# Two-level Strassen GEMMs on one core: accumulators c and d in one double bank, a new slot order and a lag of two ticks

## Chip, cores and metric

The kernel runs on one core of one Trainium2 chip. The metric is the device time of one execution in microseconds (us); the time of a kernel is the median of several runs.

## What is computed

One transformer layer over x of 8 batches x 512 tokens x 1024 features, all in float32. It has causal attention with 16 heads and rotary embedding, and a feed-forward GEMM with a LoRA term; each is wrapped in a LayerNorm before and a LayerNorm behind, and added to its input:

```python
x = x + ln(attention(ln(x)))        # q,k,v = h@Wq, h@Wk, h@Wv; rotary; causal softmax; out @ Wo
y = einsum('bsd,od->bso', ln(x), weight) + bias
lo = einsum('bsr,bor->bso', einsum('bsd,brd->bsr', ln(x), A), Bw)   # adapter by batch
x = x + ln(y + where(use_lora, lo, 0))
```

## The kernel before

The work goes through four stages. **V** (0 to about 430 us) normalizes x and multiplies it by Wv, batch by batch. The **attention** stage (about 431 to 1676 us) makes q and k, the scores, the softmax and its product with v; it has its own class `Product` (L93) and its own order PRODUCTS. **O** (about 1676 to 2020 us) multiplies by Wo, and **F** (about 2020 to 2471 us) is the feed-forward GEMM. In the program V's batches are numbered q = -8 to -1, O's 0 to 7 and F's 8 to 15.

*A batch as 49 products.* V, O and F use one scheme. The 512x1024 by 1024x1024 GEMM of a batch is computed by a two-level Strassen method: seven GROUPS (L51) at the outer level, named P1 to P7 after Strassen's products, and in each group seven sub-products SUBS, named P1 to P7 again. So a batch has N2 = 49 products. ORDER (L61) is the order of the groups in a batch, P1, P2, P4, P5, P7, P6, P3; LAST (L62) is that of the very last batch. SLOTS is the order of the seven sub-products in a group.

*Operands.* The left factors L11 to S4 are weight tiles and their sums; in V they are made on chip, for O and F they are loaded (`load_sums`, from sums made on GpSimd at L567). The right factors R11 to R22 and T1 to T4 come from the data: in V by LayerNorm (`stats_x`, `norm_x`), a transpose on TensorE (`transpose_x`, tile `ptx`, L454) and a copy on ScalarE (`keep_x`); in O and F by DMA (`load_right`). T1, T2, T4 and T3 are differences of R's, made by `sum_right` (L275) in three pieces each, on GpSimd mostly. They are written over older R's whose readers are done (`next_roles`): a batch's last group, P3, reads the last of them.

*Accumulators.* Within a group P1 and P2 accumulate into a PSUM tile a, P6 and P7 into b, P5 and P3 into c, P4 into d (SUBS). A tile is 128x256 float32. ACCS gives the buffers: a 1 (2 in O and F), b 2, c 2, d 1. `Group.product` (L302ff) opens a tile at its first product and issues two matmuls (L320, four records in the profile); in F some groups add a LoRA matmul (L327). `Group.drain` (L339ff) takes the results out: after P1 ScalarE copies a to p1 and VectorE makes u2 = b + p1; after P7 VectorE makes p1 += b, then the output quarters c + p1 and d + p1; after P2 ScalarE copies a; after P3 VectorE makes c + u2 (L342 are VectorE's adds, L347 and L354 ScalarE's copies). So TensorE's P3 adds to a c that VectorE has read in P7's drain just before. The products of slots run P6, P1, P3 of the group before, P5, P4, P7, P2: P3 of a group comes in the third slot of the next one.

*The order by hand.* `products` (L370) goes through ticks; one tick is one product. At each tick `run` (L176) issues first the events of kind "pe", then the product, then the drain of the tick before, then the other events of the tick in the order in which they were planned. Each engine takes its instructions in this order. The events are planned at fixed ticks relative to a batch's first tick, `base`: `plan_x` (V: load, statistics, norm and transposes of the next batch), COMBINE and the list in the loop over q (sums of whole groups on VectorE and GpSimd, L360), `store_v`, `plan_right` (loads and sums of the next batch's right factors), `plan_left` (F's weights, during O's last batch), `plan_rows` (O and F: row loads, the LayerNorm of the output rows, the add to the residual on GpSimd at L1109, stores, and in O a second LayerNorm with transposes on VectorE at L1118) and `plan_last` (the last batch). Loads and stores are issued on SyncE's queue (SP). O's first three groups (AHEAD) are computed in the attention stage.

*PSUM.* V uses six banks for the accumulators and two for transposes, O and F seven and one.

Of the kernel before, what the change touches and what calls it, by code (L numbers as in the profile page):

```python
# [10 lines left out]
F32 = mybir.dt.float32  # L11
# [6 lines left out]
P = 128  # L18
B, S, E = 8, 512, 1024
# [43 lines left out]
SUB = 256  # L63
# [8 lines left out]
    "P6": ("S2", "T2", "b"),  # L72
    "P7": ("S3", "T3", "b"),
}
SLOTS = ["P6", "P1", "P3", "P5", "P4", "P7", "P2"]

QK = {"P1": "A", "P2": "B", "P6": "D", "P7": "E", "P4": "F", "P5": "D", "P3": "E"}
ACCS = {"a": 1, "b": 2, "c": 2, "d": 1}
SLOT_L = {"L11": 0, "L12": 1, "S3": 2, "L22": 3, "S1": 4, "S2": 5, "S4": 6}
SLOT_R = {"R11": 0, "R21": 1, "T3": 2, "R22": 3, "T1": 4, "T2": 5, "T4": 6}  # L80

# [51 lines left out]
def sandwich_kernel(  # L133
# [161 lines left out]
    class Group:  # L295
# [9 lines left out]
        def product(self, p):  # L305
            l, r, a = SUBS[p]
            first = a not in self.acc
            if first:
                self.acc[a] = env["acc"].tile(
                    [P, SUB], F32, tag=a, bufs=2 if a == "a" and self.q >= 0 else ACCS[a], name=f"acc{a}_{self.name}"  # L310
                )
            acc = self.acc[a]
            left, right = self.W[self.L], RX[self.q, self.R][:, SLOT_R[r]]
            for k in range(2):
                stays = right[:, k, :] if self.q < B else by_blocks(right, k)
                if self.q < 0:
                    moving = left[:, SLOT_L[l], k, :]
                else:
                    moving = left[:, 4 * k : 4 * k + 4, SLOT_L[l], :]
                nc.tensor.matmul(  # L320
                    acc, lhsT=stays, rhs=moving,
                    start=(first and k == 0), stop=True, skip_group_check=True,
                )
            if self.lora and p in LORA_SUB:
                half, cols = self.lora
                i, c = LORA_SUB[p]
                nc.tensor.matmul(  # L327
                    acc, lhsT=hts[self.q - B][:, cols[c], :],
                    rhs=env["lb"][:, half * HALF + i * SUB : half * HALF + (i + 1) * SUB],
                    start=False, stop=True, skip_group_check=True,  # L330
                )
# [7 lines left out]
        def drain(self, p):  # L339

            acc, t = self.acc, self.t
            add = lambda out, x, a: nc.vector.tensor_tensor(out, acc[a], x, op=ALU.add)  # L342
            if p == "P1":
                env["u2"].reverse()
                for n, pool in (("p1", env["p1"]), ("u2", env["u2"][0])):
                    t[n] = pool.tile([P, SUB], F32, tag=n, name=f"{n}_{self.name}")
                nc.scalar.copy(t["p1"], acc["a"])  # L347
                add(t["u2"], t["p1"], "b")
            elif p == "P7":
                add(t["p1"], t["p1"], "b")  # L350
                add(self.dest(1, 1), t["p1"], "c")
                add(self.dest(1, 0), t["p1"], "d")
            elif p == "P2":
                nc.scalar.copy(self.dest(0, 0), acc["a"])  # L354
            elif p == "P3":
                add(self.dest(0, 1), t["u2"], "c")
# [13 lines left out]
    def products(q0, count, order, first=0):  # L370


        cur, before, todo = None, None, None

        def fill(q, g, p):
            nonlocal cur, before, todo
            if p == 0:
                before = cur
                cur = Group(q, order(q)[g]) if q < q0 + count else None
            name = SLOTS[p]  # L380
            group = before if name == "P3" else cur
            if group:
                group.product(name)
            if todo:
                todo[0].drain(todo[1])
            todo = (group, name) if group else None

        for n in range(first, count * N2 + 4):
            q, m = divmod(n, N2)
            g, p = divmod(m, NP)  # L390
            run(n, lambda q=q, g=g, p=p: fill(q0 + q, g, p))
# [80 lines left out]

    def plan_x(b, base):

        at(base + 10, next_roles)
        for t in range(NT):
            at(max(0, base - 12) + t, lambda t=t: load_x(b, t))
            k = (4, 5, 17, 19)[t]
            for m in range(4):
                at(base + k + m, lambda t=t, m=m: stats_x(b, t, m))  # L480
            at(base + k + 4, lambda t=t: norm_x(b, t))
        for n, k in (("R11", 11), ("R21", 18), ("R12", 25), ("R22", 32)):
            g, h = int(n[1]) - 1, int(n[2]) - 1
            for c in range(2):
                t = 2 * h + c
                at(base + k + c, lambda t=t, g=g: transpose_x(b, t, g), "pe")
                at(base + k + c, lambda pt, t=t, g=g: keep_x(b, t, g, pt), "post")
            at(base + k + 3, lambda n=n: sub_right(b - B, n, pool))
        for n, k in (("T1", 38), ("T2", 45), ("T4", 52), ("T3", 63)):
            eng = dve if n in ("T1", "T3") else pool  # L490
            for m in range(3):
                at(
                    base + k + (m if eng is dve else 0),
                    lambda n=n, m=m, eng=eng: sum_right(gvp, b - B, n, eng, slice(m, m + 1)),
                )
        for n, k in (
            ("R11", 18), ("R21", 25), ("R22", 40), ("T1", 44), ("T2", 54), ("T4", 60), ("T3", 69)
        ):
            at(base + k, lambda n=n: store_operand(b, n))
# [42 lines left out]
    for b in range(B):  # L542
        base = b * N2
        if b + 1 < B:
            plan_x(b + 1, base)
        for k, *op in COMBINE:
            at(base + k, lambda b=b, op=op: combine(b - B, *op[1:], op[0]))
        for k, tag, half, h in ((22, "c11", 0, 0), (53, "c21", 1, 0), (54, "c12", 1, 1), (57, "c22", 0, 1)):
            at(base + k, lambda b=b, tag=tag, half=half, h=h: store_v(b, tag, half, h))


    def plan_sums(pool, name, src, dst, ticks, eng=nc.gpsimd):
# [508 lines left out]
    with ExitStack() as a:  # L1061
# [88 lines left out]
            )  # L1150

        def plan_right(q, base):

            if q > 1:
                at(base + 6, next_roles)
            for n, k in (("R11", 10), ("R21", 17), ("R12", 24), ("R22", 31)):
                if q == 1 and n != "R22":
                    continue
                at(base + k, lambda n=n: load_right(gp, q, n))
                if q >= B:  # L1160
                    at(base + k + 4, lambda n=n: sub_right(q, n, nc.gpsimd, slice(0, 3)))
            if q >= B:
                for h, k in ((0, 25), (1, 39)):
                    at(base + k, lambda h=h: lora_in(q - B, h), "pe")
                    at(base + k, lambda ph, h=h: lora_keep(q - B, h, ph), "post")
                    for g in range(2):
                        at(base + k, lambda n=f"R{g + 1}{h + 1}": sub_right(q, n, nc.vector if h else nc.gpsimd, slice(3, 4)))
                at(base + 42, lambda: sub_ht(q - B))
            for n, k in (("T1", 40 if q == 1 or q >= B else 38), ("T2", 46 if q >= B else 45), ("T4", 52), ("T3", 63)):
                eng = nc.vector if q >= B and n in ("T1", "T3") else nc.gpsimd  # L1170
                for m in range(3):
                    at(
                        base + k + (m if eng is nc.vector else 0),
                        lambda n=n, m=m, eng=eng: sum_right(gp, q, n, eng, slice(m, m + 1)),
                    )

        def plan_left(base):


            for n, k in zip(("L11", "L12", "L22", "S1", "S3", "S2", "S4"), (10, 22, 34, 46, 56, 64, 72)):  # L1180
                pool = wop2 if n in ("S3", "S2", "S4") else wop
                at(base + k, lambda n=n, pool=pool: load_sums(pool, "wf", n, n))

        def plan_rows(q, base):

            for t in range(NT):
                k = base + 55 + 7 * t
                key = f"{'o' if q < B else 'y'}{q}_{t}"
# [59 lines left out]
        for q in range(NQ):  # L1248
# [4 lines left out]
                plan_left(base)  # L1253
            dve, pool = nc.vector, nc.gpsimd
            for k, e, res, l, r in (
                (18, dve, "c11", "c11", "A"), (38, pool, "c21", "c21", "c12"), (45, dve, "U", "U", "A"),
                (46, dve, "c22", "c22", "U"), (47, pool, "c21", "c21", "U"),
                (48, dve, "c12", "c12", "c22"), (52, dve, "c22", "c22", "A"),
            ) if q + 1 < NQ else (
                (18, dve, "U", "U", "A"), (31, dve, "c12", "c12", "U"), (33, dve, "U", "U", "c22"),  # L1260
                (34, pool, "c22", "c22", "c12"), (39, pool, "c11", "c11", "A"),
                (45, dve, "c21", "c21", "c12"),
            ):
                if base + k >= AHEAD:
# [100 lines left out]
```

## Time and profile before

| | us |
|---|---|
| median of 3 runs | 2475.75 |
| lowest and highest | 2475.05 and 2478.72 |
| the profiled execution | 2473.42 |
| its span | 2471.3 |

The mean granted TensorE clock of the span is 0.992. Busy times (share of the span):

| TensorE matmul | VectorE | ScalarE | GpSimd |
|---|---|---|---|
| 2361.4 us (96%) | 1782.8 us (72%) | 1046.1 us (42%) | 1518.8 us (61%) |

PE is TensorE's matmuls, PEld its weight loads, DVE VectorE, ACT ScalarE, POOL GpSimd, SP SyncE. A line `PE ptx L454 <- ACT x L420` in a list of waits means that a TensorE instruction of line 454, writing tile ptx, waited for ScalarE's write of x in line 420. In a timeline a row gives start, duration, engine, line, operation, output, inputs and shapes; a matmul's duration is modelled and overlaps with the next, so the distance between starts is the better measure.

### The profile page before, as it was taken

Reading aid. Unit: us, or ns where it says so; the run is one execution under the profiler, and the core shown is the slowest. Engines: PE = TensorE matmul, PEld = TensorE weight load, DVE = VectorE, ACT = ScalarE, POOL = GpSimd, SP = SyncE. Lnnn points to the kernel's source line nnn. Section 1 sums busy time; section 2 is a strip of 40 time slices with the busy share of each in tenths; the row PEclk is TensorE's granted clock in tenths of the full one; section 3 lists DMA queues with packets and bytes.
Section 4 is the critical chain, followed back from the end, with each engine's and each line's share of the span. In section 5 each row is a group of like instructions: output and inputs, shape, how many; then the busy total and the mean of one; then the engine's idle time right before and its main releaser. Section 6 shows DMA issues by size and latency. Waiting matters only on the chain. (4 is left out here: it accounts for less than half of the span.)

```text
span 2471.3 us, 37151 instructions
## 1 busy us (share of the span) xinstructions
PE 2361.4 (96%) x11936; PEld 1860.6 (75%) x11936; DVE 1782.8 (72%) x3942; ACT 1046.1 (42%) x2650; POOL 1518.8 (61%) x1125
## 2 busy tenths in 40 slices
PE   6999999999999999999999999799999988999997
PEld 4787887886677777777777776458888877888886
DVE  8777767384857759576685866776989988766676
ACT  3323331125555555555565566652434333222223
POOL 3878875204364553735646364776887886777674
PEclk8999999999999999999999999999999999999999
DMA  7697787998999897988989897467777698444433
GB/s 263 196 302 247 245 268 231 349 298 260 272 297 289 247 338 246 313 299 279 324 265 341 260 300 248 136 241 264 231 215 244 204 282 222 128 128 124 115 111 119
DMA packets 505650, 601.82 MB, mean 244 GB/s; under 512 B 198417, under 2 KB 344849, under 8 KB 502898
## 3 DMA queue, kind: packets, MB, share of 16 engines
q1 hardware_dynamic: 505458, 599.46, 76.7%
q8 instruction: 96, 1.57, 0.3%
q14 instruction: 96, 0.79, 0.1%
HBM read 366.55 MB, written 199.23 MB: 229 GB/s over the span
## 5 line engine op out<-in xcount | busy, mean ns | idle before, releaser
L784 ACT ACTIVATE pr<-pr,nm 128x128 f32<-128x128 f32 (+3 forms) x512 | 281.0, 550 | 187.6 <-DVE nm L774 187.5
L800 ACT ACTIVATE pr<-pr,rs 128x128 f32<-128x128 f32 x470 | 231.0, 550 | 108.9 <-DVE rs L792 108.8
L774 DVE CUSTOM_DVE_ANT_0 pr<-s,mask 128x128 f32<-128x128 f32 (+3 forms) x512 | 224.3, 484 | 42.7 <-PE s L753 40.8
L1109 POOL TENSOR_TENSOR c<-c,row 128x512 f32<-128x512 f32 x120 | 158.9, 1335 | 97.0 <-ACT c L420 79.5
L641 PE MATMUL acca_q_P<-xs,ls 128*128 128x256 f32 x896 | 217.3, 385 | 0.8 <-issue 0.8
L641 PE MATMUL accc_q_P<-xs,ls 128*128 128x256 f32 x896 | 217.0, 385 | 0.0
L641 PE MATMUL accb_q_P<-xs,ls 128*128 128x256 f32 x896 | 216.3, 384 | 0.8 <-DVE u_q_P L116 0.8
L641 PEld LDWEIGHTS acca_q_P<-xs,ls 128*128 128x128 f32 x896 | 165.3, 190 | 49.9 <-issue 21.6
L641 PEld LDWEIGHTS accc_q_P<-xs,ls 128*128 128x128 f32 x896 | 165.3, 190 | 48.2 <-issue 19.9
L641 PEld LDWEIGHTS accb_q_P<-xs,ls 128*128 128x128 f32 x896 | 165.4, 190 | 44.9 <-issue 7.7
L753 PE MATMUL s<-qk 64*128 64x128 f32 (+3 forms) x1024 | 193.0, 470 | 5.3 <-DVE nm L774 4.2
L814 PE MATMUL ptp<-ident,pr 128*128 128x128 f32 x1280 | 177.3, 277 | 11.7 <-DVE nm L774 6.0
L275 POOL TENSOR_TENSOR T<-R,T 128x512 f32<-128x512 f32 (+1 forms) x96 | 174.8, 1847 | 21.1 <-PE accc_P L320 16.9
L814 PEld LDWEIGHTS ptp<-ident,pr 128*128 128x128 f32 x1280 | 146.6, 141 | 43.3 <-ACT pr L800 14.5
L567 POOL TENSOR_TENSOR wc_g<-wc_g 128x256 f32<-128x256 f32 (+1 forms) x120 | 126.3, 1071 | 83.2 <-DMA wc_g<-in_wqk_dram 67.1
L835 PE MATMUL po<-pT,v 128*64 128x512 f32 (+3 forms) x1024 | 155.9, 443 | 9.5 <-ACT pT L829 7.3
L835 PEld LDWEIGHTS po<-pT,v 128*64 128x64 f32 x1024 | 70.6, 137 | 101.4 <-issue 65.5
L684 POOL TENSOR_TENSOR B_q<-B_q,m 128x1024 f32<-128x1024 f32 x14 | 33.1, 2365 | 176.5 <-DVE B_q L681 176.4
L829 DVE COPY pT<-ptp 128x384 f32<-128x384 f32 (+1 forms) x132 | 80.4, 614 | 39.7 <-PE ptp L814 39.7
L641 PE MATMUL accd_q_P<-xs,ls 128*128 128x256 f32 x448 | 108.7, 385 | 0.0
L753 PEld LDWEIGHTS s<-qk 64*128 64x128 f32 x1024 | 73.2, 186 | 46.7 <-issue 28.7
L567 POOL TENSOR_TENSOR wc_wo<-wc_wo 128x256 f32<-128x256 f32 (+1 forms) x64 | 66.8, 1062 | 65.1 <-DMA wc_wo<-in_wo_dram 63.4
(1116 smaller groups left out, 5739.7 us busy)
## 6 DMA issues: line engine op xcount, KB each, us to landing
ls<-wqk SPq DMA_DIRECT2D x392, 256.0 KB, 5.2
xs<-xop SPq DMA_DIRECT2D x392, 256.0 KB, 5.4
R<-attn SPq DMA_DIRECT2D x32, 896.0 KB, 6.6
wqk<-wc_g SPq DMA_DIRECT2D x16, 1568.0 KB, 9.4
x<-in_x_dram SPq DMA_DIRECT2D x32, 512.0 KB, 9.8
v<-vd SPq DMA_DIRECT2D x64, 256.0 KB, 5.4
attn<-ops SPq DMA_DIRECT2D x16, 1024.0 KB, 7.9
row<-in_x_dram SPq DMA_DIRECT2D x32, 512.0 KB, 4.4
```

The source lines that it names most:

```text
L275: eng.tensor_tensor(RX[q, n][:, c], RX[q, x][:, c], RX[q, y][:, c], op=ALU.subtract)
L567: eng.tensor_tensor(out, x, y, op=op)
L641: nc.tensor.matmul(acc[:, :, w, :], lhsT=ls[:, k, w, :], rhs=xs_[:, :, k, :], start=(first and w == 0 and k == 0), stop=True, skip_group_c ...
L684: eng.tensor_tensor(v, v, m[step - 4, q], op=ALU.add)
L753: nc.tensor.matmul(ps[:, j, at : at + L], lhsT=qT[r, qb], rhs=kT[r, : qb + 1], start=True, stop=True,)
L774: nc.vector.tensor_tensor_reduce(out=v[:, j, :], in0=self.ps[qb][:, j, :], in1=work2["mask"][:, S - L :], scale=-1.0 / HD**0.5, scalar=3.0e38,
L784: nc.scalar.activation(v[:, j, :], v[:, j, :], AF.Exp, bias=nm[:, j : j + 1], scale=-1.0, accum_out=sm[:, j : j + 1],)
L800: nc.scalar.mul(v, v, rs[:, j : j + 1])
L814: nc.tensor.transpose(pt[:, n, :], self.pr[qb][:, j, ts(kb, P)], ident)
L829: copy(self.pT[j][:, : qb + 1, ts(qb, P)], self.pt[j][:, : qb + 1, :])
L835: nc.tensor.matmul(po[j * HD : (j + 1) * HD, kb * P :], lhsT=self.v[:, kb, ts(j, HD)], rhs=self.pT[j][:, kb, kb * P :], start=(kb == 0), s ...
L1109: nc.gpsimd.tensor_tensor(c, c, row[q, t][:, ts(h, HALF)], op=ALU.add)
```

## The change

- The order of slots is P6, P1, P5, P4, P3 of the group before, P2, P7. The old order stays as CLOSING for the last group of a stage and the four ticks behind it.
- c and d are the two halves of one PSUM tile of 128x2x256 (one bank), opened by P5 with two buffers; d's first product, P4, then finds its accumulator already open and doesn't set the start flag. a and b have two buffers in all stages. In V the accumulators take six banks as before, in O and F six instead of seven.
- P7's drain reads d before c.
- LAG = 2 ticks are added to the events of `plan_x` (not to its loads), COMBINE, `store_v`, `plan_right`, `plan_left` and `plan_rows`, and to the combines of the O and F loop (in the last batch to all but its sixth). `plan_last` stays.

```diff
-SLOTS = ["P6", "P1", "P3", "P5", "P4", "P7", "P2"]
+SLOTS = ["P6", "P1", "P5", "P4", "P3", "P2", "P7"]
+CLOSING = ["P6", "P1", "P3", "P5", "P4", "P7", "P2"]
+LAG = 2
-ACCS = {"a": 1, "b": 2, "c": 2, "d": 1}
...
-            if first:
-                self.acc[a] = env["acc"].tile(
-                    [P, SUB], F32, tag=a, bufs=2 if a == "a" and self.q >= 0 else ACCS[a], name=f"acc{a}_{self.name}"
-                )
+            if a in "ab" and first:
+                self.acc[a] = env["acc"].tile([P, SUB], F32, tag=a, bufs=2, name=f"acc{a}_{self.name}")
+            elif a == "c" and first:
+                both = env["acc"].tile([P, 2, SUB], F32, tag="c", bufs=2, name=f"accc_{self.name}")
+                self.acc["c"], self.acc["d"] = both[:, 0], both[:, 1]
...
                 add(t["p1"], t["p1"], "b")
+                add(self.dest(1, 0), t["p1"], "d")
                 add(self.dest(1, 1), t["p1"], "c")
-                add(self.dest(1, 0), t["p1"], "d")
...
-            name = SLOTS[p]
+            name = (CLOSING if q + 1 >= q0 + count and (q == q0 + count or g + 1 == len(GROUPS)) else SLOTS)[p]
...
     def plan_x(b, base):
+        base += LAG
         at(base + 10, next_roles)
         for t in range(NT):
-            at(max(0, base - 12) + t, lambda t=t: load_x(b, t))
+            at(max(0, base - LAG - 12) + t, lambda t=t: load_x(b, t))
...
-            at(base + k, lambda b=b, op=op: combine(b - B, *op[1:], op[0]))
+            at(base + LAG + k, lambda b=b, op=op: combine(b - B, *op[1:], op[0]))
...
-            at(base + k, lambda b=b, tag=tag, half=half, h=h: store_v(b, tag, half, h))
+            at(base + LAG + k, lambda b=b, tag=tag, half=half, h=h: store_v(b, tag, half, h))
...
         def plan_right(q, base):
+            base += LAG
...
         def plan_left(base):
+            base += LAG
...
         def plan_rows(q, base):
+            base += LAG
...
-                (18, dve, "c11", "c11", "A"), (38, pool, "c21", "c21", "c12"), (45, dve, "U", "U", "A"),
-                (46, dve, "c22", "c22", "U"), (47, pool, "c21", "c21", "U"),
-                (48, dve, "c12", "c12", "c22"), (52, dve, "c22", "c22", "A"),
+                (20, dve, "c11", "c11", "A"), (40, pool, "c21", "c21", "c12"), (47, dve, "U", "U", "A"),
+                (48, dve, "c22", "c22", "U"), (49, pool, "c21", "c21", "U"),
+                (50, dve, "c12", "c12", "c22"), (54, dve, "c22", "c22", "A"),
...
-                (18, dve, "U", "U", "A"), (31, dve, "c12", "c12", "U"), (33, dve, "U", "U", "c22"),
-                (34, pool, "c22", "c22", "c12"), (39, pool, "c11", "c11", "A"),
+                (20, dve, "U", "U", "A"), (33, dve, "c12", "c12", "U"), (35, dve, "U", "U", "c22"),
+                (36, pool, "c22", "c22", "c12"), (41, pool, "c11", "c11", "A"),
                 (45, dve, "c21", "c21", "c12"),
```

## The prediction

> **What bounds the kernel now.** I read the page first: busy shares, slices, chain.
>
> ```profile
> PE 2361.4 (96%) x11936; PEld 1860.6 (75%) x11936; DVE 1782.8 (72%) x3942; ACT 1046.1 (42%) x2650; POOL 1518.8 (61%) x1125
> ...
> PE 22%; DVE 3%; DMA 3%; SPq 1%; POOL 0%; issue 0%; ACT 0%; ACTq 0%; DVEq 0%; POOLq 0%
> ```
>
> TensorE is busy 96% of 2471.3 us, so all that any schedule can win is the 4% in which it waits. The change removes no matmul, so only waits count. The second view is the busy time in one 50 us window each of the V, O and F stage (columns: PE, PEld, DVE, ACT, POOL, granted clock, DMA share, GB/s).
>
> ```profile
> 200.00:250.00 50.00, 48.17 (x233) 40.66 (x233) 36.15 (x67) 16.26 (x35) 39.95 (x36) 1.00 0.80 262
> 1750.00:1800.00 50.00, 48.07 (x221) 41.56 (x221) 45.76 (x98) 19.51 (x40) 42.14 (x28) 1.00 0.78 224
> 2150.00:2200.00 50.00, 50.00 (x245) 43.27 (x244) 36.38 (x68) 10.14 (x23) 35.67 (x31) 1.00 0.42 119
> ```
>
> V and O lose about 2 us in 50; settled F loses nothing. The attention stage (431 to 1676 us) has its own `Product` class and PRODUCTS order and is not touched. What the lost time waits for is in the waits of PE, first for 100 to 424 us (V), then for 1676 to 2000 us (O); columns: total, times, longest.
>
> ```profile
> PE ptx L454 <- ACT x L420: 4.1, 16, 0.4
> PE accc_-1_P L320 <- DVE c_-1_3014 L342: 2.7, 1, 2.7
> ...
> PE acca_-6_P L320 <- ACT A_-6_1100 L354: 0.8, 1, 0.8
> ```
>
> ```profile
> PE accc_P L320 <- DVE A L342: 10.9, 6, 2.0
> PE accb_P L320 <- POOL T L275: 1.6, 1, 1.6
> ```
>
> So there are three kinds: P3 waiting for P7's drain of c (accc), the single V accumulator a waiting for ACT's P2 copy (acca), and operands: transposes (ptx) and T4 from POOL. In timelines one product (four matmul records) starts 0.866 us after the one before it; I measure each loss from start to start, which adds 0.1 us to what this view lists.
>
> **Part 1: a is double in V.** It removes the acca waits: 0.92+0.10 us at five boundaries between batches (the one of 240.91 us is 0.92 start to start), and 0.95, 1.57 and 0.36 in the first two batches (31.70, 54.08, 93.75 us). Added up, 8 us. What is late next decides. At the boundary of 229 us the timeline of DVE has no gap from 229.27 to 243.06:
>
> ```profile
> 229.27 0.42 DVE L342 TENSOR_TENSOR U_-5_1755<-accc_-5_P,u_-5_P 128x256 f32<-128x256 f32 x1
> 229.72 1.94 DVE L360 TENSOR_TENSOR U_-5_1755<-U_-5_1755,A_-5_1470 128x1024 f32<-128x1024 f32 x1
> 231.69 2.17 DVE L360 TENSOR_TENSOR c_-5_1663<-c_-5_1663,U_-5_1755 128x1024 f32<-128x1024 f32 x1
> ...
> 242.84 0.21 DVE L415 TENSOR_SCALAR nb_v<-mv_v,rstd_v 128x1 f32<-128x1 f32 x1
> ```
>
> It starts when P3 of the last group ends (229.06) and ends in the LayerNorm of the next batch's first tile: ACT norms it at 243.09 to 243.91 and the transposes (ptx) start at 243.96. They stand 15 products behind that P3, so TensorE wants them 15x0.866 = 12.98 us later, at 242.04. It is 1.92 us short of that however it pays: now as 0.57 (accc), 1.02 (acca) and 0.35 (ptx), together 1.94. Take acca away and TensorE comes to ptx earlier and waits there for the same DVE chain. In the new order P3 and the transposes both move by two slots, so 15 products stay between them, and the chain holds the same combines, drains and statistics plus one: the P1 drain (u, 0.41 us, 0.34 to the next start) of the group in which the transposes fall comes before the reciprocal, where now it comes behind. So the boundary costs about 1.94+0.34, and the second ptx and later ones hardly change: **+0.4 us at each of six boundaries, +2.4 us** (bounds: -1.0 each if the norm is ready in time, +0.8 each if both pairs of transposes pay the u drain). The first batches (DVE without gap from about 40 to 72 us) gain one product of room before their first transposes: -0.5 us (-3 to +1).
>
> **Part 2: order of slots, P3 two later, c and d in one bank.** P7's drain to P3's product goes from three slots to four, P1's to P2's (a) from four to three; b stays at three; P3 to P3 stays seven. The O boundary at 1740 us, DVE, after U's drain at 1741.18:
>
> ```profile
> 1742.39 2.32 DVE L360 TENSOR_TENSOR U<-U,A 128x1024 f32<-128x1024 f32 x1
> 1744.75 2.18 DVE L360 TENSOR_TENSOR c<-c,U 128x1024 f32<-128x1024 f32 x1
> 1746.85 0.41 DVE L342 TENSOR_TENSOR p_P<-accb_P,p_P 128x256 f32<-128x256 f32 x1
> ```
>
> U's drain follows P3 of one group (ended 1740.47), the two 2.3 us combines follow it, then P7's drains, and P3 of the next group, six products (5.20 us) behind, starts at 1747.77 instead of 1745.67: 2.1 us. The combines move two ticks with P3 (45, 46 become 47, 48), so they still lie between its drain and P7's; the extra slot is no room, since P3 to P3 is what counts. U's drain starts 0.36 to 0.5 us earlier (u and a transpose are no longer in front), and d is read ahead of c, 0.34 us, and P3 needs both reads since it writes their bank. **Six waits of 2.1 us stay: 0** (-0.5 to +0.4 each, -3 to +2.4). At 2018 and 2079 us accb gives about 1.4 us to accc in the same DVE chain: 0 (±0.6). ACT's copy of p1 stands behind norms (at 1773.98 to 1778.99) with one slot less before P2: 0 (up to +0.3 for each O batch, +1.8). V's end has a gapless DVE chain from 376.59 to 404.9 and one u more: +0.3 (-2 to +2).
>
> The Trainium skill ("PSUM — Partial Sum Buffer", "PSUM bank collisions raise a hardware error") says two engines may not touch one bank and quadrant together. It speaks against the shared bank: P3 has to wait for d as well. By it the wait grows by the one read; the row for d in before is 0.41 us, 0.34 to the next start.
>
> **Part 3: LAG, two ticks = 1.73 us.** Moved are the statistics, norms, transposes and keeps of x (its loads stay), combines, V stores, R loads (SP, 896 KB, 6.6 us), wf loads and their sums (SP, POOL), the R sums (POOL), LoRA steps, and the row steps with row loads, x1 stores and output stores (SP). Consumers inside a chain move along, SP keeps its sequence, and the tiles have a batch's time. One deadline does not move: P6 of group P4, 14 slots into a batch, reads T4. POOL makes T4 in three pieces, and in O it has almost no slack:
>
> ```profile
> 1832.51 7.27 POOL L275 TENSOR_TENSOR T<-R,T 128x512 f32<-128x512 f32 x3
> 1839.74 3.48 POOL L360 TENSOR_TENSOR c<-c,U 128x512 f32<-128x512 f32 x2
> 1843.18 4.28 POOL L275 TENSOR_TENSOR T<-R,T 128x512 f32<-128x512 f32 x3
> ```
>
> T4 ends at 1847.46 and PE starts at 1847.52, 0.16 late. The seven O cases: 1713.61 (1.72 late, its R load was issued at 1687 behind the attention stores, so not by LAG), 1847.52 and 1936.88 (0.16 late each), and 1758.39, 1803.03, 1892.27, 1981.61 with 1.13 us left. The sums overwrite buffers that P3 frees (P3 two slots later) and the POOL combines and row adds before them are lagged, so T4 can come up to 1.73 us later. I take 1.65 for the two without slack and 0.2 for the four with 1.13 (0 to 0.6): **+4.1** (0, if POOL catches up in its waits for rows, 5.6 us at 1817, to 6). V has 3.7 us there except two batches with 0.7: +0.5 (0 to 2). F has 3.2 or more: 1.5 stay, 0. wf's sums and F's inputs show no wait of PE: 0.
>
> **Sum:** 2.4 - 0.5 + 0 + 0.3 + 4.1 + 0.5 = +6.8 us on the profiled execution, 2473.42 us: 2480.2. That execution is 2.33 below the median of 2475.75, so on the median's scale **2482.5 us**.
>
> **Rivals.** *Faster:* the norm chain is ready before the transposes are wanted, so the acca waits really go: 5x1.02, 0.95, 1.57, 0.36 = 8 us, and POOL catches up: -8 to -11, 2466. For it: DVE is only 72% busy in V, and ACT idle. Against: the gapless 14 us at each boundary. It decides from 2 us of slack in that chain. *Same:* POOL absorbs LAG, only the +2.4 and -0.5 stay: 2477.6. For it: POOL waits 5.6 us for a row before the chain of 1823. Against: the row load is lagged too. *Much slower:* T4's full 1.73 less its slack in O (6x1.7 = 10), V's two short batches (2), ACT's copies (1.8), and a half clock at V's end (below): +14, 2490. It decides when POOL's chain runs without gaps from the lagged row add to T4 in every batch.
>
> V ends with a wait of 2.83 us from start to start at 404.66; then matmuls take 0.43 instead of 0.216 from 406.0 to 409.4 (granted clock 0.69 in 404 to 409.5), 1.8 us lost. The 2.1 us waits of O leave the clock at 1.00. So this wait shortened below 2.1 would give 1.8 back.
>
> The Trainium skill ("TensorE: Matmul & The Clock Gate", "What's actually happening") puts the half clock after about 3.4 us idle in a free-running window. The row's 2.83 us is shorter; by the page nothing would be lost at V's end.
>
> **How the numbers follow.** A measurement of this kernel tells 0.2%, 4.95 us, from no change. Cases: slower by 5 to 10 us, 0.42 (the sum); within 5, 0.29 (unknowns of O's waits, ACT and POOL at their low bounds); faster by more than 5, 0.18; slower by 10 to 25, 0.11. The range leaves out the far half of the faster and of the much slower case: 2468.0 to 2488.0. Faster 0.18, same 0.29, slower 0.53.
>
> **What the profile after would show.** Right: no acca wait in V, but ptx waits of over 1 us at each boundary (total over 8 us instead of 4.1); accc in O still about 2 us, six times; accb on POOL's T in most O batches; no wait in settled F. Wrong: ptx waits of 0.4 as now, accc waits in O under 1 us, or T4's waits unchanged. Then the time would fall by 8 us and more.

## The result, and the profile after

The changed kernel takes 2492.03 us (median of 4 runs, 2490.30 to 2492.59) beside 2475.40 us for the kernel before (4 runs): 16.6 us more, a ratio of 1.0065 with a 95% interval of 1.0047 to 1.0082. The profiled execution took 2491.61 us with a span of 2489.8 us. The forecast was 6.8 us more, in a range of 2468 to 2488 us. It had the sign and the mechanism in O, but not the size: most of the loss is in V, at a place to which it gave nothing.

The page first: TensorE is busy for 9.8 us more (a group of four matmuls that has waited is listed with 1.13 instead of 1.03 us, one at half clock with 2.08), but the span grew by 18.5 us. The chain is followed back further than in before, so its shares can't be compared.

```profile
PE 2371.2 (95%) x11936; PEld 1866.8 (75%) x11936; DVE 1785.2 (72%) x3942; ACT 1045.8 (42%) x2650; POOL 1516.6 (61%) x1125
...
PE 61%; DMA 6%; POOL 5%; DVE 5%; ACT 2%; issue 2%; SPq 2%; ACTq 0%; POOLq 0%; DVEq 0%
```

The same windows in V, O and F (columns as before: PE, PEld, DVE, ACT, POOL, granted clock, DMA share, GB/s):

```profile
200.00:250.00 50.00, 46.72 (x228) 39.44 (x227) 35.64 (x66) 16.06 (x34) 38.50 (x34) 1.00 0.79 256
1815.00:1865.00 50.00, 48.22 (x222) 41.48 (x220) 44.43 (x99) 20.21 (x43) 41.88 (x28) 1.00 0.74 212
2180.00:2230.00 50.00, 50.00 (x245) 43.13 (x244) 33.44 (x65) 9.98 (x23) 36.84 (x31) 1.00 0.38 107
```

V lost 1.45 us in 50 us (48.17 before), O and settled F nothing. Now the waits of PE in 100 to 424 us:

```profile
PE ptx L456 <- ACT x L422: 9.4, 12, 1.0
PE accc_-1_P L322 <- DVE c_-1_2925 L344: 2.1, 1, 2.1
PE accc_-3_P L322 <- DVE c_-3_2282 L344: 1.1, 1, 1.1
...
PE accc_-4_P L322 <- DVE A_-4_2123 L344: 0.6, 1, 0.6
```

and in 1690 to 2020 us:

```profile
PE accc_P L322 <- DVE A L344: 10.5, 6, 2.0
PE accb_P L322 <- POOL T L276: 2.0, 1, 2.0
```

In V the acca waits are gone and ptx waits took their place, 9.4 us instead of 4.1: that was forecast. The line of accc_-3 <- DVE **c**_-3 was not. It is there once in each of six batches, 1.0 or 1.1 us long; it is not the wait at the boundary (that one names A), and before lost 0.2 us at this place. In O the six accc waits are what they were.

Where the time went, from the start of the same product in both traces (after minus before, us):

| up to | lead grows to | in this part |
|---|---|---|
| second batch of V | 3.4 | 3.4 |
| third batch | 5.4 | 2.0 |
| last batch (five steps of 1.3 each) | 12.0 | 6.6 |
| end of V | 11.3 | -0.7 |
| first product of attention | 12.8 | 1.5 |
| first product of O | 15.4 | 2.6 |
| O's last batch | 18.2 | 2.8 |
| F's third batch | 18.2 | 0.0 |
| last product of F | 18.9 | 0.7 |

So V's period, from one batch's first product to the next one's, went from 49.1 to 50.4 us. At the boundary (batch -4) the losses of PE add up to 2.4 us in both kernels; all of the 1.3 us is behind it, in the batch's third group. The timeline of PE there:

```profile
267.52 1.13 PE L322 MATMUL accc_-4_P<-wv_L,T_-4_1792 128*128 128x256 f32 x4 [1.02 <-DVE c_-4_1919 L344]
...
271.46 0.66 PE L456 MATMUL ptx<-ident,x 128*128 128x128 f32 x4 [0.65 <-ACT x L422]
```

From start to start the first cost 1.19 us (0.20 before) and the second 0.81 (0.56 before). What stood in front of that drain is in VectorE's timeline, of after and then of before at the same place:

```profile
258.29 0.42 DVE L344 TENSOR_TENSOR u_-4_P<-accb_-4_P,p_-4_P 128x256 f32<-128x256 f32 x1 [1.47 <-ACT p_-4_P L349]
258.63 4.38 DVE L276 TENSOR_TENSOR R_-4_1630<-R_-4_1675,R_-4_1630 128x512 f32<-128x512 f32 x3
262.94 0.41 DVE L344 TENSOR_TENSOR c_-4_1868<-accc_-4_P,u_-4_P 128x256 f32<-128x256 f32 x1
...
266.21 0.41 DVE L344 TENSOR_TENSOR p_-4_P<-accb_-4_P,p_-4_P 128x256 f32<-128x256 f32 x1
```

```profile
248.33 2.22 DVE L275 TENSOR_TENSOR R_-4_1649<-R_-4_1695,R_-4_1649 128x512 f32<-128x512 f32 x2
250.47 0.41 DVE L342 TENSOR_TENSOR u_-4_P<-accb_-4_P,p_-4_P 128x256 f32<-128x256 f32 x1
250.80 1.55 DVE L275 TENSOR_TENSOR R_-4_1649<-R_-4_1695,R_-4_1649 128x768 f32<-128x768 f32 x1
...
255.74 0.40 DVE L342 TENSOR_TENSOR p_-4_P<-accb_-4_P,p_-4_P 128x256 f32<-128x256 f32 x1
```

R <- R,R is T3 = R22 - R12, three pieces, written in place. Before, two pieces ran ahead of P1's drain (u), in time in which VectorE would have waited for ScalarE's copy of p. LAG puts T3 two slots later, behind u: VectorE now waits 1.47 us for p with nothing to do, and then does 4.38 us of T3 in one go in front of the statistics, the sum and P7's drains, on which P3 waits. This became the new theory: **T3, an operand sum on VectorE that LAG moved along, is the cost; the slots and the banks are not.** The rivals: the shared bank, the new order itself, the statistics.

### The profile page after: what moved, and what is told of

Its sections match the earlier page's. It is cut to its first block, busy times and chain, and to the rows that moved or that the text cites. A ratio compares the mean times of both kernels' runs of the same rounds, so it can differ in the third digit from the quotient of the medians.

```text
span 2489.8 us, 37117 instructions
## 1 busy us (share of the span) xinstructions
PE 2371.2 (95%) x11936; PEld 1866.8 (75%) x11936; DVE 1785.2 (72%) x3942; ACT 1045.8 (42%) x2650; POOL 1516.6 (61%) x1125
## 4 chain that ended last, share of the span: by engine, by line
PE 61%; DMA 6%; POOL 5%; DVE 5%; ACT 2%; issue 2%; SPq 2%; ACTq 0%; POOLq 0%; DVEq 0%
PE accc_P L322 8%; PE acca_q_P L644 7%; PE accb_q_P L644 7%; PE accc_q_P L644 7%; PE s L756 6%; PE accb_P L322 5%; PE po L838 5%; PE acca_P L322 5%; PE ptp L817 5%; PE accd_q_P L644 3%; POOL T L276 2%; PE accc_P L329 1%; PE ph L1141 1%; POOL wc_wo L570 1%; ACT pr L787 1%
## 5 line engine op out<-in xcount | busy, mean ns | idle before, releaser
L817 PEld LDWEIGHTS ptp<-ident,pr 128*128 128x128 f32 x1280 | 147.5, 142 | 42.4 <-ACT pr L803 13.5
L349 ACT COPY p_P<-acca_P 128x256 f32<-128x256 f32 x109 | 40.1, 368 | 156.6 <-PE acca_P L322 69.8
```

The lines of the kernel that those rows point to most:

```text
L817: nc.tensor.transpose(pt[:, n, :], self.pr[qb][:, j, ts(kb, P)], ident)
```

## The experiments

Every kernel ran beside the kernel before on the same chip. The ratio is to that, with a 95% interval; it is estimated from all the runs and need not be the quotient of the medians. Kernels from different chips are compared by their ratios.

**e1_banks: the banks alone.** The kernel before, with this edit:

```diff
-            if first:
-                self.acc[a] = env["acc"].tile(
...
+            if a in "ab" and first:
+                self.acc[a] = env["acc"].tile([P, SUB], F32, tag=a, bufs=2, name=f"acc{a}_{self.name}")
+            elif a == "c" and first:
+                both = env["acc"].tile([P, 2, SUB], F32, tag="c", bufs=2, name=f"accc_{self.name}")
+                self.acc["c"], self.acc["d"] = both[:, 0], both[:, 1]
...
+                add(self.dest(1, 0), t["p1"], "d")
                 add(self.dest(1, 1), t["p1"], "c")
-                add(self.dest(1, 0), t["p1"], "d")
```

> The kernel before with the banks alone: c and d share a double bank, a is double in V, P7's drain reads d before c; old slots, no LAG. Theory (the slots and LAG cost the 16 us, the banks do nothing): the acca waits of V go, TensorE comes to the transposes earlier and waits there for the same chain of VectorE, so the ptx waits of 100 to 424 us rise from 4.1 to about 8 us in total, the batch period of V stays at 49.1 us within 0.3, the accc waits of O stay at about 2.1, and the time is 2474 to 2478 us, within 0.1% of before. Rival A (the shared bank is what costs): P3 waits 0.34 us more at every group and the time is above 2485. Rival B (a's second buffer really saves): V's period falls by 1 us a batch, the time is 2466 to 2469.

Measured: 2483.46 us, ratio 1.0030 (1.0018 to 1.0042). The waits of V and of O:

```profile
PE ptx L455 <- ACT x L421: 0.8, 5, 0.2
PE accc_-5_P L321 <- DVE A_-5_1448 L343: 0.6, 1, 0.6
...
PE accc_-5_P L321 <- DVE A_-5_1764 L343: 0.6, 1, 0.6
```

```profile
PE accc_P L321 <- DVE A L343: 13.5, 6, 2.3
```

V's period is 49.1 us, what it was: a second buffer for a, with the one bank for c and d that makes room for it, saves nothing in V, as the theory says. But it is not ptx that takes the wait here (0.8 us in all); it is accc, 0.80 us from start to start twice at the boundary and 0.53 in the third group. The run does not tell a second buffer that saves nothing from one whose saving the shared bank takes back. In O the six accc waits grew from 1.72 to 2.12 us to 2.41 to 2.43. The four that were 2.07 us or more grew by the read of d (0.34 us) for which P3 now waits too. Behind three of the six TensorE fell to half clock for 3 us, some 1.5 us lost each. The waits and half clocks are some 7 us together; other waits of O got shorter, and the lead over before grows by 4.4 us from O's second batch to its last and by 4.9 more up to F's fourth, where two more waits end in half clock. The two traces are 9.4 us apart, the medians 5.5, so the sum is rough. The time lies between the theory's and rival A's: the shared bank does cost, in O.

**e2_order: slots and LAG with the old accumulators** (the lines of the diff on accumulators and on P7's drain left out).

> The changed kernel with the accumulators of before (a single in V, c and d in banks of their own, c drained before d), with the new slots and LAG. Theory (slots and LAG cost): V's period is 50.4 us or more as in the changed kernel, with acca waits added again or not, the time 2488 to 2496 us. Rival A (the shared bank costs): about 2476 to 2480 us. If a's second buffer helps only with the new slots, it is above 2496.

Measured: 2515.85 us, ratio 1.0155 (1.0139 to 1.0170). It falls into the case above 2496, but not for that case's reason: a costs 0.4 us a batch in the list, d 2.8. The new lines in V:

```profile
PE accd_-4_P L322 <- DVE c_-4_1950 L344: 1.9, 1, 1.9
...
PE accd_-4_P L322 <- DVE A_-5_1788 L344: 0.9, 1, 0.9
```

d has one buffer here, and the new order puts P4 in the slot before P3: its product now waits for P7's drain, one slot earlier than P3 would. From the third batch on V's period is 50.4 us three times and 52.1 twice, where half clock follows the wait. V, O and F all lose, 19, 11 and 13 us in the two traces. So the banks cost 0.3% in the old order and save 0.9% in the new one; each half of the change alone is worse than before.

**e3_t3: the changed kernel, T3 of V at its old ticks.**

```diff
-        for n, k in (("T1", 38), ("T2", 45), ("T4", 52), ("T3", 63)):
+        for n, k in (("T1", 38), ("T2", 45), ("T4", 52), ("T3", 63 - LAG)):
```

> The changed kernel with the sums of T3 in V at their old ticks (63 to 65, not 65 to 67), so that VectorE makes them before P1's drain again and not in one piece of 4.4 us behind it. Theory (LAG puts T3 in front of the next P7 drain): the accc wait of the third group of a V batch (1.0 us in the list, 1.29 us start to start) falls to 0.3 or less, V's period from 50.4 to about 49.4 us, and the time by about 7 us, to 2483 to 2487. Rival (P3 waits there for the statistics and the combine that stand in front of P7's drain whatever T3 does): no change, 2490 to 2493.

Measured: 2480.50 us, ratio 1.0015 (1.0007 to 1.0024), where the changed kernel has 1.0065: 0.5%, 12 us. V's window and VectorE at the same place:

```profile
200.00:250.00 50.00, 48.38 (x239) 41.39 (x238) 36.18 (x69) 17.92 (x38) 40.66 (x37) 1.00 0.82 269
```

```profile
250.15 2.22 DVE L276 TENSOR_TENSOR R_-4_1630<-R_-4_1675,R_-4_1630 128x512 f32<-128x512 f32 x2
252.30 0.41 DVE L344 TENSOR_TENSOR u_-4_P<-accb_-4_P,p_-4_P 128x256 f32<-128x256 f32 x1
252.63 1.55 DVE L276 TENSOR_TENSOR R_-4_1630<-R_-4_1675,R_-4_1630 128x768 f32<-128x768 f32 x1
...
257.28 0.41 DVE L344 TENSOR_TENSOR p_-4_P<-accb_-4_P,p_-4_P 128x256 f32<-128x256 f32 x1
```

T3 is two pieces, u, one piece again; both waits in the third group are gone, not only that of accc, which is why the gain is above the 7 us expected. V's period is 48.26 us, 0.8 less than before: with T3 in its place the new scheme does save in V.

**e5_t3late: the same edit the other way round**, T3 two ticks later (65 for 63) in the kernel before.

> The kernel before with one thing changed: the sums of T3 in V two ticks later (65 to 67 instead of 63 to 65), as LAG puts them. Theory (T3's 4.4 us of VectorE, moved from the idle time before P1's drain to behind it, are what makes V slower): V's period rises from 49.1 to between 50.0 and 51.3 us and the time by 6 to 14 us. Rival (T3 late does harm only together with the new slots): the period stays within 0.3 us of 49.1 and the time within 2 us of before.

Measured: 2488.21 us, ratio 1.0050 (1.0031 to 1.0069), 13 us. V's period is 51.1 us (50.6 in two of the six steps), and the third group shows new waits (before lost 0.20 us at accc there and nothing at acca):

```profile
PE acca_-4_P L320 <- ACT c_-4_1968 L354: 1.0, 1, 1.0
PE accc_-4_P L320 <- DVE c_-4_1968 L342: 0.7, 1, 0.7
```

Taken out of the changed kernel and put into the one before, T3's two ticks are worth the same 0.5%. That cause is shown, and it doesn't need the new slots.

**e4_stats: the changed kernel, statistics and norms of two tiles early.**

```diff
-            at(max(0, base - LAG - 12) + t, lambda t=t: load_x(b, t))
-            k = (4, 5, 17, 19)[t]
+            soon = b > 1 and t < 2
+            at(max(0, base - LAG - 12 - 14 * soon) + t, lambda t=t: load_x(b, t))
+            k = (4, 5, 17, 19)[t] - 17 * soon
```

> The changed kernel with the loads of the first two x tiles of a V batch 14 ticks earlier and their statistics and norms 17 ticks earlier (from the third batch on), where VectorE stands idle. Theory (after a batch boundary TensorE waits for the chain of combines, drains, statistics and norm on VectorE): the first ptx wait of each boundary (1.1 us) goes, the accc waits stay at 0.6 to 1.0, V's period falls by 0.5 to 1.2 us in each of six batches, the time is 2484 to 2489. If the period falls by over 2 us a batch, the statistics also cause the second accc wait: below 2480. Rival (the transposes wait for ACT or for PSUM, not for the statistics): no change, 2490 to 2493.

Measured: 2495.09 us, ratio 1.0072 (1.0058 to 1.0086): no gain. The first ptx wait is gone (ptx 3.9 us in all), and this came in its place:

```profile
PE acca_-4_P L322 <- ACT p_-4_P L349: 1.9, 1, 1.9
...
PE acca_-5_P L322 <- ACT p_-5_P L349: 1.3, 1, 1.3
```

Neither theory was right. The transposes did wait for the statistics, but the early norms (four of 0.75 us) stand on ScalarE in front of P1's copy, here for the wait of batch -5:

```profile
240.18 1.52 ACT L422 ACTIVATE x<-x,nb_v,rstd_v 128x512 f32<-128x512 f32 x2 [0.79 <-DVE nb_v L417]
241.60 0.35 ACT L349 COPY p_-5_P<-acca_-5_P 128x256 f32<-128x256 f32 x1
```

**e10_v_stats: the same with the norms behind P1's copy**, in the kernel that has the new scheme in V alone (e6, below) and the mended hand-over (e12, below): `- 19 * soon` and the norms at `base - LAG - 5`.

> The new scheme in V alone (O and F as before), T3 at its old ticks, with two edits: in V's last batch the sums from tick 45 on without LAG, and the statistics of the first two x tiles 19 ticks earlier, their norms at slot 2, behind P1's copy on ScalarE (from the third batch on). Theory: the ptx wait of 1.1 us goes and no acca wait comes in its place, V's period falls from 48.3 to 46.9 to 47.4 us; the hand-over wait falls from 2.5 to about 1.0 us; time 6 to 10 us under the V-only kernel without these two, 0.1 to 0.3% below before. Rival (a wait of the same size returns at accc or acca, as it did with statistics and norms both early): the period stays at 48.0 us or more, time within 3 us of the V-only kernel.

Measured: 2490.89 us, ratio 1.0062 (1.0047 to 1.0077), worse than without. The statistics now come before their data:

```profile
232.45 0.69 DVE L411 BATCH_NORM_STATS2 bn_v<-x 128x6 f32<-128x512 f32 x1 [4.69 <-DMA x<-in_x_dram]
```

The load had not landed, and VectorE stood still for 4.69 us with the drains queued behind (26.9 us in 100 to 380 us). The run says nothing on statistics whose data are there, and shows again what a waiting instruction at the head of VectorE's queue costs. **e11_all** adds the sums of e9 (below) to it.

> The two kernels beside this one put together: V with its statistics early and its last sums without LAG, O and F of before with the three sums spread out. If both theories hold, the gains add: 10 to 20 us under before. If the rivals hold, within 4 us of before.

Measured: 2485.87 us, ratio 1.0044 (1.0028 to 1.0059): the loss of e10 less the gain of e9.

**e6_v_only: the new scheme in V, T3 in place, O and F as before.**

> New banks, slots and LAG in V alone, with T3 at its old ticks; O and F as in the kernel before. Theory: V's period is 48.3 us, 0.8 less than before, in the batches from the third on, first batch and hand-over to the attention stage cost 3 us and 1.5 us more as in the changed kernel, O and F (435 to 436 us for F) as before; time 2473 to 2478 us, so 2 to 5 below the run with the new O and F. Rival (O and F gain from their new slots): above 2481.

Measured: 2478.32 us, ratio 1.0018 (1.0004 to 1.0031), where e3 with its new O and F has 1.0015. I had expected 2 to 5 us less than e3; slots, banks and LAG together cost or save nothing in O and F that these two intervals, of some 3 us either way, could show.

**e12_closing: e3 with the last sums of V not lagged.**

```diff
-            at(base + LAG + k, lambda b=b, op=op: combine(b - B, *op[1:], op[0]))
+            at(base + LAG * (b + 1 < B or k < 45) + k, lambda b=b, op=op: combine(b - B, *op[1:], op[0]))
```

> The changed kernel with T3 of V at its old ticks and the sums from tick 45 on in V's last batch without LAG: that batch's last group has the old slots, so with LAG two sums (1.7 and 1.2 us) stand on VectorE in front of the last drain. Theory: the wait of the attention stage's first product falls from 2.5 to about 1.0 us and the half clock behind it goes, 1.5 to 3 us under the kernel with T3 alone, within 0.1% of before. Rival (that product waits for its load): the wait stays at 2.3 us or more.

Measured: 2473.56 us, ratio 0.9999 (0.9988 to 1.0010). The hand-over in the changed kernel, VectorE and then PE:

```profile
440.62 1.71 DVE L362 TENSOR_TENSOR c_-1_2991<-c_-1_2991,U_-1_3084 128x1024 f32<-128x1024 f32 x1
442.43 1.23 DVE L362 TENSOR_TENSOR c_-1_3018<-c_-1_3018,c_-1_2991 128x1024 f32<-128x1024 f32 x1
443.57 0.42 DVE L344 TENSOR_TENSOR A_-1_3113<-accc_-1_P,u_-1_P 128x256 f32<-128x256 f32 x1
```

```profile
444.20 1.97 PE L644 MATMUL acca_q_P<-xs,ls 128*128 128x256 f32 x8 [2.31 <-issue]
```

and in e12:

```profile
427.52 1.21 DVE L362 TENSOR_TENSOR c_-1_3018<-c_-1_3018,c_-1_2991 128x1024 f32<-128x1024 f32 x1
428.82 0.42 DVE L344 TENSOR_TENSOR A_-1_3116<-accc_-1_P,u_-1_P 128x256 f32<-128x256 f32 x1
```

```profile
429.45 1.75 PE L644 MATMUL acca_q_P<-xs,ls 128*128 128x256 f32 x7 [0.67 <-DMA ls<-wqk]
```

V's last group keeps the old slots, its last drain comes two ticks earlier than elsewhere, but LAG moved the sums as if it did not: two of them stand in front of it. The profile names no releaser at 444.20 ("issue"), and in e12 a load, but in all fourteen traces the attention stage's first product starts 0.21 to 0.24 us after the end of V's last drain: 443.99 and 444.20 here, 429.24 and 429.45 in e12, 431.18 and 431.39 in before. So it waits for the drain, and the rival (its load) is out. The wait itself fell by 1.6 us, about as expected; the time fell by more (0.16%, 4 us), but the two intervals overlap a little, so that size is rough. With this and T3 mended the change is neither faster nor slower than before.

**e7_c22late: one sum of O and F behind P7's drain** in the kernel before: (46, c22 += U) becomes 48, (48, c12 += c22) becomes 49.

> The kernel before with one sum moved in O and F: c22 += U (2.2 us on VectorE) two ticks later, behind P7's drain, and c12 += c22 one tick later. Theory (the accc wait of 2.1 us at each O boundary is P7's drain queued behind both 1024-wide sums, whatever the distance in slots): the six accc waits go or fall below 0.3 us, the two at 2018 to 2086 us shorten too, the time falls by 8 to 14 us, to 2464 to 2470. Rival (something else, as the transposes or the row statistics, then holds VectorE up by as much): it moves less than 4 us.

Measured: 2474.93 us, ratio 0.9999 (0.9987 to 1.0010). O's waits:

```profile
PE accb_P L320 <- DVE u_P L342: 11.1, 8, 1.7
PE accc_P L320 <- DVE A L342: 1.6, 6, 0.7
```

The rival had the size, and VectorE as the engine, but it is neither transposes nor statistics: the 10.9 us of accc became 11.1 of accb, P1's drain now being the one that queues behind two sums. **e8_both** does the same to e3, in V too.

> The changed kernel with T3 of V at its old ticks and with c22 += U one tick later, behind P7's drain, in V, O and F. Theory: V's first accc wait of each boundary (0.80 us) goes and its ptx wait grows by as much, V's period stays 48.3; in O the six accc waits of 1.9 to 2.1 us go, accb on POOL's T stays at 0.2 to 0.5 us or grows to 1; time 8 to 14 us under the run with T3 alone, 2467 to 2473 us. Rival (in O POOL's T4 takes the whole of the gain, since TensorE then comes 2 us earlier to it): accb on T grows to 2 us a batch and the time stays above 2477.

Measured: 2485.02 us, ratio 1.0037 (1.0022 to 1.0051): accb 13.5 us in O in place of accc's 10.6, and about 1 us a batch in settled F that e3 hasn't. The rival had the time (above 2477) but named POOL; it was VectorE again.

**e9_spread: three sums spread out** in O and F of the kernel before: c22 += U at tick 48, c12 += c22 at 51, c22 += A at 54.

> The kernel before with three sums of O and F spread out: c22 += U at tick 48 (was 46), c12 += c22 at 51 (was 48), c22 += A at 54 (was 52). The move of c22 += U alone gave accb waits of 1.85 us at the boundary in place of the accc waits. Theory (VectorE's work is dense there, and what is next in its queue waits; only work moved into idle time of VectorE shortens it): the accc and accb waits of O fall from 2.1 to between 0 and 1.0 us a batch, the time by 5 to 12 us. Rival (VectorE has no idle time left in O, 92% busy): waits of 1.5 us or more a batch come back at another place, the time within 3 us of before.

Measured: 2469.21 us, ratio 0.9974 (0.9961 to 0.9986), the one version that beats both kernels:

```profile
PE accc_P L320 <- DVE A L342: 4.8, 7, 0.9
PE accb_P L320 <- POOL T L275: 3.4, 2, 2.2
PE accb_P L320 <- DVE u_P L342: 2.7, 2, 2.1
```

No drain has two sums in front of it any more. accc fell from 10.9 to 4.8 us; T4 took 1.8 of it back (3.4 beside 1.6). But the sums did not only move, they also got shorter: VectorE's thirty 1024-wide sums from 1735 to 1990 us take 49.5 us here, 57.6 in before and 58.3 in e7, while GpSimd's sums of the same line take 40.8 instead of 35.9. What makes the same sum take 1.2 or 2.6 us these runs do not separate, so how much of the gain is the spreading and how much the shorter sums stays open.

## Why the prediction was wrong

- **a's second buffer saves nothing at the boundary, the wait moves to ptx: right.** The acca waits are gone and V's boundary costs 2.4 us as before (+0.06, not +0.4). e1 adds that it may move to accc as well.
- **"the second ptx and later ones hardly change": wrong, and this is the step that failed.** Behind it stands part 3, which lists "the R sums (POOL)" and lets consumers move along. T1 and T3 of V are VectorE's, and T3's 3.8 to 4.4 us stand in the queue in front of drains that move by other amounts. I priced LAG by data (who needs T4) and not, for VectorE, by what each moved instruction passes. Size: 0 in the sum, 12 us by e3 and e5.
- **V's end +0.3:** the 2.83 us wait shrank to 2.26 + 0.61 and the half clock went (-0.7), but the hand-over (+1.5 in this trace) was not foreseen. e12 against e3: 0.16%, 4 us.
- **First batches -0.5 (-3 to +1):** +3.4, outside the bounds. In every kernel with the new slots and LAG the second batch starts at 89 us or later, in every one without at 86. T3 in place doesn't change it. VectorE's work there is not without gap in before, as part 1 has it: it stands still 0.8 us at 43.0 and 2.2 us at 70.1. The largest new wait there is one of 2.8 us at 37 us: P2 waits for ScalarE's copy of P1, which is one slot nearer in the new order. No run isolates it, so the cause is open.
- **O: six accc waits stay: right** (10.5 us beside 10.9). **T4 +4.1:** the mechanism was right, the size too large. POOL ends 0.05 us ahead of PE in six of the seven batches now, but the waits are 0.33 us in five of them, not 1.65 in two; TensorE itself comes later.
- **Settled F 0, the two accb waits at its start 0:** right within 1 us, the second only net (-2.8, then +2.1 and +0.7).
- **"The 2.1 us waits of O leave the clock at 1.00":** true of the trace of before, wrong as a rule, see below.
- **Not in the sum:** another 2.6 us in the attention stage, whose code is the same. From its first product to O's first one behind it (1676.4 us in before) it takes 1242.4 to 1245.0 us in the eight kernels whose hand-over has no lagged sums (before, 1245.0, among them) and 1242.7 to 1249.0 in the six that have them (after 1247.6). Four of the six are above all of the eight, two are not; it is one execution of each, and whether this part goes with the hand-over is not shown.

By medians and ratios the account closes with two terms: T3's 0.5% and 0.16% for the hand-over with what may follow it are the 0.65%. What is left (0.8 us saved in each of V's later batches, 3.4 us lost in its first) nets to nothing that can be measured.

## What to carry to other kernels

When a schedule is shifted by a constant, go through every instruction that shifts, engine by engine, and write down what it now stands in front of and behind in its queue; a sum with ample time by its data can still sit in front of a drain that hasn't any. A wait at an engine that is dense around it (VectorE at a batch boundary) was moved here, not removed, by buffers, slots or the order of two sums; it got shorter only in e9, where no drain was left with two sums in front of it and the sums themselves took less. And where a constant lag assumes a new order, the places that keep the old one need the old ticks.

## What the runs showed of the hardware

A wait of 2.1 to 2.4 us may or may not halve TensorE's clock. None of O's six in before did (1.72 to 2.12 us), none of five in after (1.86 to 1.88), but the one of 2.12 us at 1765.4 in after did, and three of six at 2.41 to 2.43 us in e1; matmuls then start 0.43 us apart for 3 us. Here are two waits of the same length, first in before, where the clock stayed, then in after, where it did not:

```profile
1747.77 1.13 PE L320 MATMUL accc_P<-wo_S,R 128*128 128x256 f32 x4 [1.96 <-DVE A L342]
```

```profile
1765.39 1.13 PE L322 MATMUL accc_P<-wo_S,R 128*128 128x256 f32 x4 [1.96 <-DVE A L344]
```

The granted clock of 1764 to 1771 us in after:

```profile
1764.00:1771.00 7.00, 5.61 (x18) 4.61 (x19) 6.93 (x12) 0.74 (x2) 7.00 (x4) 0.76 0.77 183
```

It is the last figure but two, 0.76.

What decides is where the wait falls. In each of the fourteen traces the half-clock stretches between 100 us and the last product are 3.41 us long or twice that, and start whole multiples of 3.41 us apart. Cut V, O and F from 100 to 2440 us into these windows and add up, in each at full clock, the time in which no matmul streams (one of 128x256 counted as 0.217 us, the distance of starts at full clock). With 2.12 us or more the next window is at half clock in all 52 cases, with 2.05 us or less in none of 4344; of four cases in between two are. The wait that ends at 1765.39 in after lies whole in the window from 1763.3 to 1766.7 (2.20 us idle). The one that ends at 1747.77 in before is cut by the window's end at 1747.45 and leaves 1.80 us in front of it.

The Trainium skill ("TensorE: Matmul & The Clock Gate", "What's actually happening") gives half clock after a whole idle window of some 3.4 us, in windows that run free. The free-running window of 3.41 us is in these traces; but 2.1 us of idle time in one were enough.
